# New slots in a hand-ordered plan: y times silu(z) and the norms' variances one slot later, plans of their own for the MLPs of images 5 to 7 and for the first unit

## The chip, the cores and the metric

The kernel runs on one NeuronCore of a Trainium2 chip. What counts is the device time of one execution in microseconds (us). It is told as the median of three runs, beside one execution that the hardware profiler recorded.

## What is computed

The input is a batch of 8 images of 384 channels and 32 x 32 pixels, in float32. Four layers follow one another. Layer 0 is a Mamba block with a residual. Layer 1 is a Mamba block whose output is scaled by a gate (attention pooling over the image, then two small products), with a residual, and then an MLP with a residual. Layers 2 and 3 are depthwise 13 x 13 convolutions with folded batch norms, and a pointwise product between them. Cut to what matters here:

```python
xn  = (x - mean) * rsqrt(var + 1e-5) * ln_w + ln_b       # norm over the 384 channels
xin, z = split(xn @ in_proj_w.T)                         # 768 channels each
u   = silu(conv4(xin) + conv_b)                          # causal, 4 taps
dt_lo, B, C = split(u @ x_proj_w.T)                      # 24 ranks, 16 + 16 states
delta = softplus(dt_lo @ dt_proj_w.T + dt_proj_b)
h   = h * exp(delta * A) + delta * u * B                 # a scan over 1024 pixels, 16 states
y   = (sum over states of h * C + u * D) * silu(z)
out = y @ out_proj_w.T + x
...
xs = xs + mo * (1 + mod)                                 # layer 1, behind its Mamba block
h  = gelu(ln(xs) @ fc1_w.T + fc1_b) @ fc2_w.T + fc2_b    # 384 -> 1536 -> 384
xs = xs + h
```

## The kernel before

**Units and items.** The work of both Mamba layers is cut into 32 units: a layer, an image and one half of its pixels (512). Their order is layer 0 of images 0 and 1, then alternately layer 1 of image b-1 and layer 0 of image b+1, and at the end layer 1 of images 6 and 7. Each unit has 48 items: 6 blocks of 128 channels (d) times 8 items (n), where an item is a tile of 128 x 1024 numbers (32 channels times 4 states on the partitions, two quarters of the channels along the free side). One slot of the plan belongs to one item, so scans run in slots 0 to 1535.

**What each slot issues.** The loop at the end of `layers` goes through the slots K. All engines' orders are written out by hand: within an engine, instructions run in the order in which the program issues them. In slot K the loop issues `fold` (every second slot: PE adds the two finished items K-2 and K-1 into `acc`, L574; with the first pair of a block also the product with D, L571), `keep` (ACT stores the last state, L560; for the items named in `AT["pool"]` POOL multiplies h by C, L563), `decay` of item K+1 (ACT, two exponentials, L516), `inflow` of item K+2 (POOL, L523), `scan` of item K (DVE, L544 or L547, and for the items not in `AT["pool"]` also h times C, L552), and then everything that the plan holds for slot K: first what was put with `first=True`, then the rest, each in the order in which it was put.

**Buffers that matter.** `hc`, the product of h and C, has 3 buffers in SBUF, used in turn by DVE's and POOL's products. `acc` is one PSUM buffer: L571 of the next block starts it anew, after `y_out` (L579, DVE, acc times silu(z)) has read the old one. `f`, for the MLP's products, is one PSUM buffer too: ACT has to take each one out (L690) before the next begins. `mm` has two PSUM buffers. `sq`, the square of the centred input, has one buffer.

**The plan.** `AT` is a table of slots. Unit i's preparation (norm, in-projection L406, shift and convolution L416 to L437, ranks L460, step sizes L482, z) stands in the slots of unit i-1; its output products (L595) in those of unit i+1. A norm is a chain: load (L361), mean on PE (L366), centring on DVE (L369), three squares on ACT (L375), each followed at once by its product with 1/384 on PE (L376), then ACT and POOL steps. Step sizes go to DRAM (`flat`, L496) and come back repeated over partitions (`repeat`, L505); both are DMAs of SP's queue.

**MLP.** Each half image passes through the MLP as one piece of the plan: a norm, 12 up slices of 3 products (L686) at `pace_up` slots each, four batches of gelu (L447), then 3 down outputs of 12 products (L699) at `pace_down` slots each. A half starts when the half before it is through and its unit has ended. `mlp_plan` has the numbers: (pace_up, first down slot, pace_down, slots of the gelu batches, gap). Before, plan 0 serves images 0 to 6, plans 2 and 3 the two halves of image 7, and plan 1 is not used.

**The first unit.** Negative slots come before the first scan, and there is nothing in them but the plan: the weights of the in-projection are multiplied by the norm's gain (`fold_product`, `fold_scale`, L343 to L353), stored to DRAM (`fold_store`, L356) and loaded from there by `slice_in` (L311), also for the first unit. Besides, `prepare` makes the filter tables of the convolutions in pieces, one to a slot from slot -40: batch norms, a bias regrouped through DRAM (`by_group` L140, `grouped` L145), `spread` (L150, PE and ACT), and six tables (loads L194, DVE, store L216).

Of the kernel before, what the change touches and what calls it, by code (L numbers as in the profile page):

```python
# [16 lines left out]
P = 128  # L17
# [93 lines left out]
def prepare(nc, k, vec, a, dram, tile, mm, got):  # L111
# [65 lines left out]
    yield  # L177
    for n, quad in zip(("b2", "b3"), quads):
        spread(n, quad)
    yield  # L180
# [4 lines left out]
    for name in ("k2", "k3"):  # L185
        got[name] = dram.tile([C, 4, HK, KP], F32, name=f"{name}_rows")
        for c in range(KC):
# [29 lines left out]
            yield  # L217

AT = {'in_ahead': 3, 'out_ahead': 2, 'taps_ahead': 4, 'norm': (-5, -2, -1, 0, 1, 2, 3, 3, 4, 5, 7, 8, 12, 12, 13), 'x': (14, 16, 18, 24, 26, 29), 'shift': 1, 'conv': 4, 'u': 5, 'silu': ((28, 3, 0), (34, 6, 0), (40, 6, 4), (57, 6, 6)), 'hid': 2, 'ranks': (33, 34, 35), 'z': (31, 35, 37, 38, 40, 41), 'B': (41, 43, 46, 47), 'C': (44, 46, 47, 50), 'repeat': (9, 12, 12, 13), 'out': (0, 4, 9), 'out_half': 3, 'out_add': 4, 'out_gate': 2, 'res_ahead': 1, 'heads': 15, 'softmax': (16, 17, 18), 'attend': (19, 24, 27, 26), 'context': 28, 'hidden': (28, 29, 32, 35, 36, 39), 'gates': (43, 40, 45), 'mlp': 22, 'mlp_norm': (-7, 0, 1, 1, 2, 3, 4, 4, 4, 6, 6, 10, 11, 11, 12), 'mlp_plan': ((3, 60, 12, (21, 33, 44, 69), -2), (1, 48, 7, (20, 24, 44, 48), -2), (2, 46, 6, (18, 30, 36, 46), -2), (1, 36, 4, (22, 30, 36, 36), -2)), 'fold0': (-22, -13), 'fold0_step': (1, 2), 'shifted': 1, 'bc_out': 36, 'store': 2, 'px_ahead': 2, 'pool': (0, 6), 'norm0': (-98, -18, -16, -15, -14, -13, -12, -11, -10, -10, -9, -8, -8, -3, -3), 'soft': ((37, 2), (45, 4), (62, 6)), 'du': 1, 'du_pace': 0, 'flat_u': 2, 'inject': 0, 'prepare': (-40, 4),
# [3 lines left out]
def layers(tc, k, a, vec, x0, x1, x2, x3, lasting, got):  # L225
# [11 lines left out]
    PIECES = 27  # L237
# [4 lines left out]
    with ExitStack() as st:  # L242
# [69 lines left out]

        def slice_out(s, m, src):
            s.w["out", m] = work.tile([P, KD, P], F32, tag="wo", name="wo", bufs=3)
            nc.sync.dma_start(s.w["out", m], src)
# [55 lines left out]
        def square(s, c):  # L371
            if c == 0:
                s.var = mm()
            sq = work.tile([P, T], F32, tag="sq", name="sq", bufs=1)
            nc.scalar.activation(sq, s.xt[:, c], AF.Square)  # L375
            nc.tensor.matmul(s.var, k["avg"], sq, start=c == 0, stop=c == KC - 1)  # L376
# [340 lines left out]
        def norm(s, src, tag, at, slots):  # L717
# [5 lines left out]
            for c in range(KC):  # L723
                put(next(slots), square, s, c)
# [18 lines left out]
        for j, s in enumerate(folds):  # L743
            for m in range(2 * KD):
                at = (j - 1) * SLOTS + 7 + 2 * m if j else AT["fold0"][m // KD] + AT["fold0_step"][m // KD] * (m % KD) - SLOTS
                use_in(at, s, m, s.src[m])
                put(at, fold_product, s, m)
                put(at + 1, fold_scale, s, m, first=True)
                put(at + 2, fold_store, s, m)

# [7 lines left out]
        for i, s in enumerate(units):  # L758

            lay, at = s.layer, (i - 1) * SLOTS  # L760
            norm(s, lay.src[s.b], "xt", at, AT["norm"] if i else AT["norm0"])
            for d in range(KD):
                e = at + AT["x"][d]
                use_in(e, s, d, lay.w_in[d])
# [7 lines left out]
            for j, (e, u1, z1) in enumerate(AT["silu"]):  # L772
# [3 lines left out]
                put(at + e, table, batch, AF.Silu)  # L776
                u0, z0 = u1, z1
            for e, d1 in AT["soft"]:
# [9 lines left out]
            put(at + AT["ranks"][0] - 6, load_xp, s)  # L788
            put(at + AT["ranks"][0], ranks, s, (0, 1, 2))
            put(at + AT["ranks"][1], ranks, s, (3, 4, 5))  # L790
            put(at + AT["ranks"][2], ranks_out, s, first=True)
            for d, e in enumerate(AT["z"]):
                use_in(at + e, s, KD + d, lay.w_in[KD + d])
                put(at + e, product, s, KD + d)
                put(at + e + 1, raw_z, s, d, first=True)
            put(at + AT["bc_out"], bc_out, s)
# [375 lines left out]
```

## Time and profile before

| | us |
|---|---|
| runs: median of 3 | 6992.39 |
| lowest, highest | 6982.28, 6993.99 |
| the profiled execution | 6987.24 |
| its span, first to last instruction | 6985.1 |
| TensorE's granted clock, mean | 0.919 |
| first scan starts | 142.56 |
| last y times silu(z) starts | 6120.42 |

The page gives, per engine, the time in which it was busy and its share of the span. A wait is named by the instruction that stood and by the one that released it, so `DVE u L579 <- PE acc L574` is DVE standing before line 579 until a product of line 574 was done; behind it stand the total, the number of times and the longest. In a window's line the first numbers are its bounds and length, then busy time (and count of instructions) of PE, PEld (weight loads), DVE, ACT and POOL, then TensorE's clock, the share of the DMA engines and GB/s.

### The profile page before, as it was taken

The page shows a single profiled execution, that of the slowest core. Times are in us where ns is not written, and L with a number is a line of the kernel's source. Part 1 is how long each engine was busy: PE and PEld are TensorE (multiplying, and loading weights), DVE is VectorE, ACT ScalarE, POOL GpSimd, SP SyncE. Part 2 cuts the span into 40 slices and gives each one's busy share as a digit, 9 for nine tenths or more (in the row PEclk, how much of TensorE's full clock was granted, in tenths as well). Part 3 has the DMA queues.
Part 4 walks back from the last instruction along what each step waited for, and adds up shares of the span by engine and source line. Part 5 has one row for each costly group of instructions (what it writes and reads, how often), then busy time and mean ns, then how long its engine had stood idle before and what let it go on. Part 6 is the DMA issues. An engine that isn't in the chain of part 4 may idle for free. (4 is left out here: it accounts for less than half of the span.)

```text
span 6985.1 us, 78481 instructions
## 1 busy us (share of the span) xinstructions
PE 5945.9 (85%) x22562; PEld 2089.5 (30%) x22562; DVE 5843.5 (84%) x4975; ACT 4472.7 (64%) x7478; POOL 5427.6 (78%) x3146
## 2 busy tenths in 40 slices
PE   6887787888888888889888888888888989777898
PEld 2222222222322232223222232223222323134545
DVE  3899998898888889888988989889998888903849
ACT  4776666767676767767676767676777767422222
POOL 2888888888898878888888888888888788804626
PEclk7888889999999999999999999999999999899999
DMA  5655555566656565666656665666565666425979
GB/s 141 173 166 156 153 163 149 162 168 173 174 160 180 154 181 162 168 163 173 165 163 166 169 180 160 171 167 181 158 176 164 174 163 171 131 67 139 263 223 241
DMA packets 962291, 1171.95 MB, mean 168 GB/s; under 512 B 314248, under 2 KB 554440, under 8 KB 961864
## 3 DMA queue, kind: packets, MB, share of 16 engines
q1 hardware_dynamic: 789576, 1064.75, 56.2%
q10 hardware_dynamic: 147712, 55.08, 3.0%
q0 software_dynamic: 24576, 47.12, 2.3%
q8 instruction: 184, 3.01, 0.2%
q14 instruction: 243, 1.99, 0.1%
HBM read 911.75 MB, written 204.21 MB: 160 GB/s over the span
## 5 line engine op out<-in xcount | busy, mean ns | idle before, releaser
L523 POOL TENSOR_TENSOR dbu<-B,ru 128x1024 f32<-128x1024 f32 x1536 | 3589.8, 2359 | 193.9 <-DVE h L547 75.9
L516 ACT ACTIVATE h<-rd,A 128x512 f32<-128x512 f32 x3072 | 2120.8, 691 | 826.2 <-DVE hc L552 613.1
L544 DVE TENSOR_TENSOR_SCAN h<-h,state,dbu 128x512 f32<-128x512 f32 x1152 | 1482.4, 1287 | 97.1 <-POOL delta L491 40.9
L552 DVE TENSOR_TENSOR hc<-h,C 128x1024 f32<-128x1024 f32 x1152 | 1411.1, 1225 | 110.7 <-PE acc L574 19.3
L547 DVE TENSOR_TENSOR_SCAN h<-h,dbu 128x1024 f32<-128x1024 f32 x576 | 1318.4, 2289 | 157.6 <-ACT h L516 127.8
L574 PE MATMUL acc<-hc,fold 128*32 128x512 f32 x6144 | 1152.9, 668 | 259.8 <-DVE hc L552 214.4
L563 POOL TENSOR_TENSOR hc<-dbu,C 128x1024 f32<-128x1024 f32 x384 | 904.0, 2354 | 529.2 <-DVE dbu L544 224.5
L406 PE MATMUL mm<-xt,wi 128*128 128x512 f32 x2304 | 1195.3, 660 | 94.8 <-ACT delta L482 25.7
L686 PE MATMUL f<-mx,wi 128*128 128x512 f32 x1152 | 625.6, 648 | 157.4 <-ACT fh L690 76.2
L699 PE MATMUL f<-fh,wo 128*128 128x512 f32 x1152 | 617.8, 648 | 116.9 <-DMA wo<-in_fc_dram 46.0
L406 PEld LDWEIGHTS mm<-xt,wi 128*128 128x128 f32 x2304 | 449.9, 207 | 821.8 <-issue 569.9
L595 PE MATMUL mm<-u,wo 128*128 128x512 f32 x1152 | 555.7, 620 | 30.1 <-DMA wo<-in_l_out_dram 28.3
L544 DVE TENSOR_TENSOR_SCAN dbu<-h,state,dbu 128x512 f32<-128x512 f32 x384 | 470.6, 1268 | 23.9 <-ACT h L516 14.2
L574 PEld LDWEIGHTS acc<-hc,fold 128*32 128x32 f32 x6144 | 163.4, 112 | 1091.3 <-DVE hc L552 482.7
L547 DVE TENSOR_TENSOR_SCAN dbu<-h,dbu 128x1024 f32<-128x1024 f32 x192 | 438.0, 2281 | 20.7 <-ACT h L516 11.2
L956 PE MATMUL ps<-xp,wt 128*32 128x256 f32 x6144 | 378.9, 389 | 61.0 <-DVE xp L951 37.9
L932 POOL DMA_DIRECT2D xp<-x x384 | 212.8, 558 | 278.5 <-DMA x<-q_out 139.2
L430 PE MATMUL mm<-xp,taps 128*64 128x512 f32 x1536 | 413.8, 661 | 17.9 <-ACT xp L416 9.6
L486 POOL TENSOR_TENSOR delta<-delta,u 128x512 f32<-128x512 f32 x192 | 241.2, 1266 | 231.4 <-ACT delta L482 228.8
L686 PEld LDWEIGHTS f<-mx,wi 128*128 128x128 f32 x1152 | 214.1, 202 | 541.7 <-issue 276.4
L306 ACT ACT_TABLE_LOAD x289 | 370.8, 1283 | 5.8 <-PEq L1160 0.7
L416 ACT ACTIVATE xp<-mm,b_in 64x512 f32<-64x512 f32 x384 | 261.7, 681 | 166.9 <-PE mm L406 163.0
(142 smaller groups left out, 5783.9 us busy)
## 6 DMA issues: line engine op xcount, KB each, us to landing
ru<-uu SPq DMA_DIRECT2D x1536, 128.0 KB
rd<-dd SPq DMA_DIRECT2D x1536, 128.0 KB
wi<-w_in SPq DMA_DIRECT2D x384, 192.0 KB
xp<-xp SPq DMA_DIRECT2D x384, 128.5 KB
dd<-delta SPq DMA_DIRECT2D x192, 256.0 KB
uu<-delta SPq DMA_DIRECT2D x192, 256.0 KB
wo<-in_l_out_dram SPq DMA_DIRECT2D x96, 384.0 KB
wi<-fc_w SPq DMA_DIRECT2D x192, 192.0 KB
```

Source lines behind the costliest of these rows:

```text
L406: nc.tensor.matmul(s.ps[m], w[:, c], s.xt[:, c], start=c == 0, stop=c == KC - 1)
L430: nc.tensor.matmul(s.ps[d][64 * h : 64 * h + 64], taps[:, h, j], xp[h][:, 2 * j : 2 * j + T], start=j == 0, stop=j == 1,)
L516: nc.scalar.activation(y[:, q], s.dr[d][1][h][:, q], AF.Exp, scale=s.layer.A[:, at : at + 1])
L523: nc.gpsimd.tensor_tensor(dbu, s.B[g].unsqueeze(1).to_broadcast([P, 2, T]), s.ur[d][1][h], ALU.mult)
L544: nc.vector.tensor_tensor_scan(to[:, q], y[:, q], dbu[:, q], first, ALU.mult, ALU.add)
L547: nc.vector.tensor_tensor_scan(flat_to, flat_y, flat_b, first, ALU.mult, ALU.add)
L552: nc.vector.tensor_tensor(hc, to, s.C[g].unsqueeze(1).to_broadcast([P, 2, T]), ALU.mult)
L563: nc.gpsimd.tensor_tensor(hc, y, s.C[g].unsqueeze(1).to_broadcast([P, 2, T]), ALU.mult)
L574: nc.tensor.matmul(s.acc[d][32 * r : 32 * r + 32], k["fold"], tiles[r // 2][:, r % 2], start=False, stop=n == PER - 2)
L595: nc.tensor.matmul(s.ps[m], w[:, d], s.us[d], start=d == 0, stop=d == KD - 1)
L686: nc.tensor.matmul(s.ps[m], s.w["in", m][:, c], s.xt[:, c], start=c == 0, stop=c == KC - 1)
L699: nc.tensor.matmul(s.down, s.w["out", 2 * m + f // KD][:, f % KD], s.hs[f], start=f == 0, stop=f == KF - 1)
```

## The change

The arithmetic is the same; the order and some buffers change.

- `y_out` is put at `AT["y"]` = 25 instead of 24: one slot later, after the second scan of the next block.
- POOL multiplies items 0 and 4 of each block by C, instead of 0 and 6.
- `square` is split: the product with 1/384 is now `variance`, put one slot after the square, ahead of the plan's other entries of that slot.
- `fold` is issued after the scan of the slot instead of at its start.
- `mlp_plan` gets five plans: images 0 to 4, image 5, image 6, and the two halves of image 7. `mlp_raw` is put at a slot computed otherwise, which is the same one for paces 1, 2 and 3.
- For the first unit, the twelve weight slices are loaded into buffers of `u` and `zs`, all at one early slot, scaled there and handed to the products from there (`slice_first`, `lend`); they are still stored to DRAM for later units. The first unit's preparation has a table of slots of its own (`first`, `norm0`), and the second unit's norm too (`norm1`). `prepare` has `spread` as its last piece, and one piece fewer.
- A number of other slots move by one or a few.

`AT` is a single line in the file; its changed entries are shown one to a line.

```diff
-'norm': (-5, -2, -1, 0, 1, 2, 3, 3, 4, 5, 7, 8, 12, 12, 13)
+'norm': (-5, -2, -1, 0, 1, 2, 3, 3, 5, 5, 7, 7, 11, 12, 13)
-'silu': ((28, 3, 0), (34, 6, 0), (40, 6, 4), (57, 6, 6))
+'silu': ((28, 3, 0), (34, 6, 0), (40, 6, 3), (57, 6, 6))
-'z': (31, 35, 37, 38, 40, 41), 'B': (41, 43, 46, 47), 'C': (44, 46, 47, 50)
+'z': (31, 34, 36, 38, 40, 41), 'B': (40, 43, 47, 48), 'C': (42, 45, 47, 52)
-'out': (0, 4, 9), 'softmax': (16, 17, 18), 'attend': (19, 24, 27, 26)
+'out': (0, 5, 9), 'softmax': (17, 18, 19), 'attend': (19, 22, 25, 26)
-'hidden': (28, 29, 32, 35, 36, 39), 'gates': (43, 40, 45)
+'hidden': (29, 30, 32, 35, 36, 39), 'gates': (47, 41, 46)
-'mlp_norm': (-7, 0, 1, 1, 2, 3, 4, 4, 4, 6, 6, 10, 11, 11, 12)
+'mlp_norm': (-7, 0, 1, 2, 3, 4, 5, 5, 5, 6, 6, 10, 10, 12, 12)
-'mlp_plan': ((3, 60, 12, (21, 33, 44, 69), -2), (1, 48, 7, (20, 24, 44, 48), -2),
-             (2, 46, 6, (18, 30, 36, 46), -2), (1, 36, 4, (22, 30, 36, 36), -2))
+'mlp_plan': ((3, 62, 12, (21, 31, 42, 69), -2), (2, 42, 6, (26, 30, 42, 46), -2),
+             (2, 40, 4, (24, 26, 34, 40), -2), (2, 40, 3, (24, 26, 34, 36), -2),
+             (2, 42, 7, (22, 28, 36, 36), -2))
-'fold0': (-22, -13), 'fold0_step': (1, 2), 'bc_out': 36, 'pool': (0, 6), 'flat_u': 2
+'fold0': (-145, -128), 'fold0_step': (1, 7), 'bc_out': 37, 'pool': (0, 4), 'flat_u': 1
-'norm0': (-98, -18, -16, -15, -14, -13, -12, -11, -10, -10, -9, -8, -8, -3, -3)
+'norm0': (-97, -89, -86, -85, -83, -80, -77, -75, -74, -73, -72, -71, -69, -69, -68)
+'norm1': (-3, -1, 0, 1, 2, 3, 4, 4, 8, 8, 10, 10, 12, 13, 13)
+'y': 25, 'fold': 0, 'var': 1, 'down_gap': 0
+'first': {'x': [2, 4, 7, 10, 13, 16], 'silu': [[14, 3, 0], [22, 6, 0], [34, 6, 2], [44, 6, 6]],
+          'ranks': [22, 24, 25], 'z': [29, 31, 31, 33, 34, 35],
+          'soft': [[29, 2], [33, 4], [60, 6]], 'bc_out': 29,
+          'B': [32, 34, 36, 39], 'repeat': [0, 0, 0, 1], 'C': [38, 43, 43, 46]}
```

```diff
 def prepare(nc, k, vec, a, dram, tile, mm, got):
...
     quads = [grouped(n, f) for n, f in zip(("b2", "b3"), flats)]
-    yield
-    yield
-    for n, quad in zip(("b2", "b3"), quads):
-        spread(n, quad)
     yield
...
             nc.sync.dma_start(got[name][c * P : (c + 1) * P], rows)
             yield
+    for n, quad in zip(("b2", "b3"), quads):
+        spread(n, quad)
+    yield
...
+        def slice_first(s, m, src):
+
+            tag, bufs = ("u", 12) if m < KD else ("zs", 7)
+            t = work.tile([P, T], F32, tag=tag, name=tag, bufs=bufs)
+            s.w["in", m] = t[:, 0 : KC * P].rearrange("p (c m) -> p c m", m=P)
+            nc.sync.dma_start(s.w["in", m], src)
...
         def square(s, c):
+            sq = work.tile([P, T], F32, tag="sq", name="sq", bufs=1)
+            nc.scalar.activation(sq, s.xt[:, c], AF.Square)
+            s.sq = {c: sq}
+
+        def variance(s, c):
             if c == 0:
                 s.var = mm()
-            sq = work.tile([P, T], F32, tag="sq", name="sq", bufs=1)
-            nc.scalar.activation(sq, s.xt[:, c], AF.Square)
-            nc.tensor.matmul(s.var, k["avg"], sq, start=c == 0, stop=c == KC - 1)
+            nc.tensor.matmul(s.var, k["avg"], s.sq.pop(c), start=c == 0, stop=c == KC - 1)
...
             for c in range(KC):
-                put(next(slots), square, s, c)
+                e = next(slots)
+                put(e, square, s, c)
+                put(e + AT["var"], variance, s, c, first=AT["var"] > 0)
...
-                at = (j - 1) * SLOTS + 7 + 2 * m if j else AT["fold0"][m // KD] + AT["fold0_step"][m // KD] * (m % KD) - SLOTS
-                use_in(at, s, m, s.src[m])
+                at = (j - 1) * SLOTS + 7 + 2 * m if j else AT["fold0"][m // KD] + AT["fold0_step"][m // KD] * (m % KD)
+                put(at - AT["in_ahead"] if j else AT["norm0"][0] - SLOTS, slice_in if j else slice_first, s, m, s.src[m])
...
+        def lend(s, m):
+            s.w["in", m] = folds[0].w["in", m]
...
-            norm(s, lay.src[s.b], "xt", at, AT["norm"] if i else AT["norm0"])
+            first = AT if i else {**AT, **AT["first"]}
+            norm(s, lay.src[s.b], "xt", at, AT["norm"] if i > 1 else AT[f"norm{i}"])
             for d in range(KD):
-                e = at + AT["x"][d]
-                use_in(e, s, d, lay.w_in[d])
+                e = at + first["x"][d]
+                if i:
+                    use_in(e, s, d, lay.w_in[d])
+                else:
+                    put(e, lend, s, d)
...
             for d in range(KD):
                 at = i * SLOTS + (d - 2) * PER
-                for e, (which, h) in zip(AT["repeat"], (("u", 0), ("d", 0), ("u", 1), ("d", 1))):
+                slots = AT["first"]["repeat"] if i == d == 0 else AT["repeat"]
+                for e, (which, h) in zip(slots, (("u", 0), ("d", 0), ("u", 1), ("d", 1))):
                     put(at + e, repeat, s, d, which, h)
                 put(at + 12, load_skip, s, d)
-                put(at + 24, y_out, s, d, first=True)
+                put(at + AT["y"], y_out, s, d, first=True)
...
-                pace_up, down, pace_down, tables, gap = AT["mlp_plan"][max(b - B + 2, 0) + (b == B - 1) * (1 + half)]
+                pace_up, down, pace_down, tables, gap = AT["mlp_plan"][max(b - B + 4, 0) + (b == B - 1) * half]
...
-                    put(e + pace_up, mlp_raw, s, m, first=True)
+                    put(e + 2 * pace_up // KC + 1, mlp_raw, s, m, first=True)
...
             for K in range(min(plan.slots), n_items + 1):
-                if K > 0 and K % 2 == 0:
-                    fold((item(K - 2), item(K - 1)))
...
                     scan(item(K))
-                plan.run(K)
+                if AT["fold"]:
+                    plan.run(K)
+                if K > 0 and K % 2 == 0:
+                    fold((item(K - 2), item(K - 1)))
+                if not AT["fold"]:
+                    plan.run(K)
```

## The prediction

> **What bounds the kernel now.** I read the page's busy shares first, then the chain of waits (to cut the span into stages), then the windows of those stages, the waits of each engine between the first and the last scan, and last the timeline around single waits.
>
> ```profile
> PE 5945.9 (85%) x22562; PEld 2089.5 (30%) x22562; DVE 5843.5 (84%) x4975; ACT 4472.7 (64%) x7478; POOL 5427.6 (78%) x3146
> ```
>
> Two engines are nearly full, so the stages decide. The timeline of DVE has the first scan at 142.56 and the last y times silu(z) (L579) at 6120.42. The windows (busy time of PE, PEld, DVE, ACT, POOL, then clock and DMA) of the prologue, of units 26 to 31 (each ends at its sixth L579) and of the three stretches after the last scan:
>
> ```profile
> 0.00:142.50 142.50, 94.82 (x240) 43.78 (x240) 27.55 (x121) 62.08 (x136) 17.91 (x24) 0.78 0.49 137
> ```
> ```profile
> 5003.30:5179.90 176.60, 153.89 (x470) 48.73 (x469) 159.19 (x98) 140.48 (x245) 154.76 (x75) 0.96 0.61 169
> 5179.90:5374.50 194.60, 167.24 (x487) 53.55 (x486) 172.75 (x145) 126.44 (x193) 163.06 (x84) 0.93 0.62 165
> 5374.50:5563.10 188.60, 169.84 (x553) 60.46 (x552) 168.38 (x122) 141.82 (x252) 155.02 (x75) 0.92 0.65 176
> 5563.10:5757.30 194.20, 169.64 (x491) 54.23 (x490) 173.09 (x145) 128.41 (x196) 163.11 (x84) 0.92 0.62 166
> 5757.30:5942.30 185.00, 167.94 (x545) 58.90 (x544) 166.64 (x121) 143.23 (x254) 155.02 (x75) 0.92 0.62 171
> 5942.30:6120.40 178.10, 125.63 (x328) 33.16 (x326) 168.60 (x143) 82.85 (x118) 142.37 (x66) 0.81 0.46 123
> ```
> ```profile
> 6120.40:6204.00 83.60, 71.64 (x157) 29.63 (x158) 5.20 (x7) 20.03 (x26) 0.00 (x0) 0.98 0.33 83
> 6204.00:6308.00 104.00, 77.75 (x158) 29.98 (x156) 4.44 (x4) 28.85 (x38) 7.88 (x7) 0.90 0.28 71
> 6308.00:6408.00 100.00, 73.56 (x152) 27.54 (x150) 2.86 (x5) 28.85 (x38) 37.26 (x46) 0.95 0.33 83
> ```
>
> The reader is to see three regimes: 142.5 us in which no engine is full; 5978 us of scans, DVE about 90% busy and PE close behind; and 288 us of MLP alone (6120 to 6408), where DVE and POOL stand still. The 577 us of depthwise convolutions behind are untouched. What DVE waits for between 142 and 6120 (us in total, times, longest):
>
> ```profile
> DVE u L579 <- PE acc L574: 172.4, 89, 5.8
> DVE h L547 <- ACT h L516: 127.8, 83, 3.0
> DVE h L544 <- POOL delta L491: 40.9, 30, 3.4
> ...
> DVE hc L552 <- PE acc L574: 19.3, 30, 2.4
> ```
>
> The first is the costliest, and the timeline shows one of its causes:
>
> ```profile
> 3021.92 2.07 PE L376 MATMUL mm<-sq,avg 128*128 128x512 f32 x2 [3.56 <-ACT sq L375]
> ...
> 3023.93 1.94 PE L574 MATMUL acc<-hc,fold 128*32 128x512 f32 x8
> ...
> 3025.93 0.69 DVE L579 TENSOR_TENSOR u<-acc,zs 128x512 f32<-128x512 f32 x1 [2.42 <-PE acc L574]
> ```
>
> PE stood 3.56 us before a variance product, since ACT had not yet squared; the fold queued behind it ended late, and DVE stood 2.42 us before L579. PE loses 110.4 us to this wait in the scans (L376 on L375).
>
> **What the Trainium skill says.** "TensorE: Matmul & The Clock Gate", Part 2, Step-by-step: matmuls stay in program order, only weight loads are pulled ahead; the three lines above agree, the fold did not pass the waiting variance. "Perfetto Trace Analysis", Identifying the Most-Contended Engine: busy matmul time is a poor measure of distance from PE's limit. So I take a unit with 91% (167.94 of 185.00) as nearly full, not as full. "DMA: Bandwidth & Descriptors", Two DMAs through the same engine are not ordered: a DMA that reads what another wrote must wait for its completion. SP does so here, standing from 48.3 (a load of taps comes between) to 55.5:
>
> ```profile
> 46.88 0.90 SPq L140 DMA_DIRECT2D b_flat<-fh  x2
> ...
> 55.53 0.93 SPq L145 DMA_DIRECT2D fh<-b_flat  x2
> ```
>
> **Part 1: y one slot later, POOL's products at items 0 and 4, variance one slot later.** No instruction is added. L579 moves behind scan 1 and product hc 1 of the next channel block. It cannot gain a whole slot: hc has 3 buffers, and hc 1 reuses that of hc 6, which the same fold frees. So DVE will wait for that fold at hc 1 (L552). That comes one scan (2.29 us, L547) later than L579 did. Listing the 90 waits of L579 (173.6 us over the whole trace), the part up to 2.3 us of each sums to 141.6, and 32 remain. More of the cause goes too: POOL's hc 6 no longer stands before this fold (PE waits 42.8 us for L563), and the 110 us before variances. The moved wait of the variance itself has 3.9 us (5978/1536 items) more to be met. Against it: acc is one buffer, so the skip product (L571, two records of 0.59, 1.2 us) of the next block now waits for L579 (0.68) behind hc 1, where it ran early. Behind it on PE stand the fold of items 0 and 1 and whatever the plan has. Where PE was waiting for hc 1 anyway this delays PE 0.68 + 1.2 = 1.9 us per block; where PE is late, nothing. Its 192 blocks bound it by 365 us, and by 0. I take 60 us given back, between the two: PE waits for DVE at L574 159 times, but most such moments have slack behind them. Net -80, range -140 to +100. The fold call's new place behind the scan changes no engine's order (only fold and plan issue to PE). flat_u one slot earlier makes SP wait for POOL's product sooner; L496 waits 162 us for it now without DVE waiting for the result (no DMA among DVE's main waits); the other moved slots I cost at 0 with it.
>
> **Part 2: MLP plans of images 5, 6, 7.** By the code's arithmetic the halves start at slots 1222, 1318, 1414, 1510, 1606, 1668 before; after at 1222, 1280, 1414, 1464, 1514, 1561. Scans end at 1536. Before, one half and its ups from slot 1536 on, then two more halves lie behind; after, one half less: the half that ran from 6204 to 6308 moves under scans, 104 us. What stands at 6120 is otherwise the same (5 of 12 ups done, the same output products). Besides, 4 of the down products before it follow the last norm's mean, not 2: 2 x 0.95 us more of that norm hidden. Sum -106, range -98 to -114.
>
> The displaced work: a half is 36 up and 36 down products of 0.95 us and 9 of the norm, 77 us. Spread over slots by each plan's pace (34 us over the ups, 34 over the downs, 9 at the start) it changes the PE load of units 25 to 31 by about +7, +27, +19, -34, -13, +38, +31. Unit 26: 154 + 27 = 181 in 176.6, so some +13; unit 27 +2; unit 30: 168 + 38 = 206, at 96%, which no window shows yet, about 215, +30; unit 31: 157 in 178, +2; units 28 and 29 relieved, -10 each. Sum +27, range 0 to +60.
>
> **Part 3: the first unit.** The twelve weight slices stay in SBUF (buffers of u and zs), so the products no longer wait for a round trip through w_in (4.5, 3.7 and 0.9 us at L406), and spread, for which PE stood 10.5 us, goes to the end. Against it, 12 x 0.45 us of slice loads now precede x in SP's queue: x lands about 19 instead of 14, the norm ends about 44 instead of 39. Then SP decides. The slots put the loads and stores of five of the six filter tables (7.9, 7.9, 7.7, 7.1, 5.8 us each in SP's timeline, L194 to L216) ahead of the flats. Product 3 ends about 65 (44 + 4 x 3.3 of L406 at the early clock + 2 x 2.5 of L430 + 3 for the first shift to land); SP meets the round trip (8.6 us) and starts the tables near 76; 5 of them, 36 us: the first flat at 112, against 114.85. From there to the scan it was 27.7 us, of which 9.8 SP stood before the third ru and a 768 KB load of the next x competed; both now come later, and I count 13. First scan at 125: -18, range -35 to 0.
>
> **Sum** against the profiled run (6987.24; its span 6985.1): -80 - 106 + 27 - 18 = -177, 6810. The median of the runs, 6992.4, lies 5 above that run, inside their spread of 12, so I say 6810.
>
> **Rivals.**
> - The wait merely moves (L579's 173 becomes L552's, or PE cannot run above 91%): part 1 gives -25. For it: L552 waits for the same fold. Against: DVE comes there 2.3 us later, and most waits are shorter. 6987 - 25 - 106 + 27 - 18 = 6865.
> - PE saturates in units 26, 27, 30, 31 and the displaced half comes back: crowding +80 instead of +27. For it: 206 of load in 185. Against: units 28 and 29 are idle enough. 6987 - 80 - 106 + 80 - 18 = 6863.
> - Everything hidden: nothing given back by the skip product (-140), crowding +10, start -30: 6987 - 140 - 106 + 10 - 30 = 6721.
> - Slower: the skip product. If PE is the bound in steady units and every block costs it 1.9 us: +365 - 142 = +223; 6987 + 223 - 106 + 27 - 18 = 7113. It decides once the give-back exceeds 142 + 106 + 18 - 27 = 239 us, 1.24 us per block. For it: PE's 91%. Against: PE idles 17 to 27 us per unit in the windows of 26 to 30, and the wait costs only where PE was ahead.
>
> That the change does not act is excluded: the slots are executed as written.
>
> **How the numbers follow.** Forecast 0.50, first rival 0.20, second 0.13, all hidden 0.10, slower 0.07. Range 6715 to 6890: it takes in the cases at 6721, 6865 and 6863 with the ends of the start and tail terms, and leaves out the slower one. What a measurement can tell from no change is 0.2%, 14 us. Faster 0.91, same 0.02, slower 0.07.
>
> **What would show it.** Right: L579 waits under 40 us, L552 on acc 30 to 80; L376's wait on L375 nearly gone; last L579 to the last MLP store about 182 us; unit 30 longer than 200; first scan near 125. Wrong: L571 waiting for L579 by hundreds of us with DVE waits growing elsewhere; a tail above 200; a first scan after 142, with SP standing at the filter tables.

## The result, and the profile after

The changed kernel takes 6950.82 us (median of 4 runs, 6940.02 to 6954.78), the kernel before 6991.66 in the same series (6982.28 to 6993.99). The ratio is 0.9942 with an interval of [0.9924, 0.9959]: about 41 us or 0.6% faster, where 6810 was forecast. The time lies above the upper end of the range, 6890. The profiled execution took 6954.78 us, its span 6952.9, at a mean clock of 0.926.

The busy line of the page of after, to be held against that of before:

```profile
PE 5904.4 (85%) x22562; PEld 2097.6 (30%) x22562; DVE 5851.6 (84%) x4975; ACT 4475.0 (64%) x7478; POOL 5429.7 (78%) x3146
```

The same work is done, and the two full engines stand at the same shares. The stages tell more. Windows of after (bounds, length, then busy PE, PEld, DVE, ACT, POOL, clock, DMA): the prologue, units 26 to 30, and the stretch behind the last y times silu(z), which starts at 6196.99:

```profile
0.00:133.30 133.30, 92.36 (x234) 42.96 (x234) 26.43 (x121) 65.57 (x141) 22.01 (x25) 0.81 0.44 130
...
5026.90:5230.70 203.80, 180.56 (x521) 60.37 (x521) 162.60 (x101) 146.00 (x253) 163.02 (x83) 0.92 0.63 165
5230.70:5427.70 197.00, 178.58 (x527) 59.62 (x526) 171.76 (x144) 139.13 (x209) 156.59 (x78) 0.95 0.64 166
5427.70:5616.30 188.60, 161.00 (x489) 54.93 (x487) 167.97 (x122) 125.48 (x229) 154.22 (x75) 0.83 0.61 166
5616.30:5805.60 189.30, 159.31 (x462) 48.87 (x462) 171.41 (x143) 131.52 (x201) 162.12 (x85) 0.94 0.59 158
5805.60:6021.30 215.70, 197.24 (x619) 72.29 (x620) 174.15 (x126) 149.91 (x265) 164.03 (x83) 0.94 0.65 169
...
6197.00:6280.00 83.00, 73.74 (x162) 30.42 (x162) 6.94 (x8) 26.27 (x35) 0.00 (x0) 0.98 0.33 86
6280.00:6372.50 92.50, 71.85 (x144) 27.99 (x144) 1.50 (x2) 26.15 (x34) 34.78 (x41) 0.91 0.34 79
```

Cutting both spans at the first scan and at each unit's sixth y gives the ledger, in us:

| stage | before | after | difference | prediction |
|---|---|---|---|---|
| prologue, to the first scan | 142.56 | 133.30 | -9.3 | -18 |
| unit 0 | 184.1 | 203.9 | +19.8 | 0 |
| units 1 to 25 | 4676.7 | 4689.7 | +12.9 | -80 |
| units 26 to 31 | 1117.1 | 1170.1 | +53.0 | +27 |
| last y to the last MLP output (L705, L714 after) | 287.5 | 175.5 | -112.0 | -106 |
| the rest | | | +3 | 0 |
| span | 6985.1 | 6952.9 | -32.2 | -177 |

The tail came as worked out. The steady units gave nothing (their +13 us is less than what a sum of 25 units differs by from one profile to the next, as the last section shows). Yet the wait on which their gain was put is gone. Waits of after between the first scan and the last y (waiting engine and line, releaser: us in total, times, longest). L588 is the old L579, L553 and L556 are the scans, L561 hc, L580 the skip product, L379 the square, L385 the variance:

```profile
DVE h L556 <- ACT h L525: 182.4, 111, 5.8
...
PE acc L580 <- DVE u L588: 153.5, 84, 4.9
ACT sq L379 <- PE mm L385: 151.6, 62, 5.4
...
DVE h L553 <- ACT h L525: 79.6, 44, 4.5
...
DVE xt L375 <- PE mm L372: 20.9, 4, 20.0
...
DVE hc L561 <- PE acc L583: 14.5, 14, 2.3
...
PE mm L385 <- ACT sq L379: 8.2, 8, 2.0
```

VectorE's 173.5 us before y are down to 1.2, and TensorE's 110.4 us before variances are down to 8.2. In their place VectorE waits 262 us for ScalarE's decays (L553 and L556 together; 163 before, L544 and L547), TensorE 153.5 us before the skip product (1.7 before), and ScalarE 151.6 us before squares (14.3 before). The lines named h leave out the scans of the two items that GpSimd multiplies by C, whose output is named dbu; with them VectorE waits 300 us for decays where it waited 189. Another 69 us before scans (2 before) have no releaser in the profile. In units 1 to 25 all of VectorE's waits sum to 387 us before and 386 us after: there the wait for y went elsewhere in full.

ScalarE's wait before squares is new in kind, and the timeline of after shows one case (start, duration, engine and line, then the idle time before it and its releaser):

```profile
3030.84 0.62 ACT L379 ACTIVATE sq<-mx 128x512 f32<-128x512 f32 x1
3032.13 1.42 ACT L525 ACTIVATE h<-rd,A 128x512 f32<-128x512 f32 x2 [0.67 <-DVE hc L561]
3037.61 0.63 ACT L379 ACTIVATE sq<-mx 128x512 f32<-128x512 f32 x1 [4.06 <-PE mm L385]
...
3032.75 1.90 PE L580 MATMUL acc<-u,skip 128*128 128x512 f32 x2 [4.44 <-DVE u L588]
3034.58 1.93 PE L583 MATMUL acc<-hc,fold 128*32 128x512 f32 x8
3036.44 1.13 PE L385 MATMUL mm<-sq,avg 128*128 128x512 f32 x2
```

TensorE stood 4.44 us for y, so the variance behind the fold came at 3036.44. It frees the only `sq` buffer, and ScalarE stood 4.06 us before the next square, with the next decay queued behind it (3038.14). Two of the edits meet here: y late holds up TensorE, the variance late ties ScalarE to TensorE. VectorE did not stand for that decay at once, though: its scans at 3036.40 and 3040.25 started without a wait. So this case shows how ScalarE is held, and not yet that VectorE's waits for decays come from it.

### The profile page after: what moved, and what is told of

Read it like the earlier page. It is cut to its first block, busy times and chain, and to the rows that moved or that the text cites. A ratio compares the mean times of both kernels' runs of the same rounds, so it can differ in the third digit from the quotient of the medians.

```text
span 6952.9 us, 78464 instructions
## 1 busy us (share of the span) xinstructions
PE 5904.4 (85%) x22562; PEld 2097.6 (30%) x22562; DVE 5851.6 (84%) x4975; ACT 4475.0 (64%) x7478; POOL 5429.7 (78%) x3146
## 5 line engine op out<-in xcount | busy, mean ns | idle before, releaser
L553 DVE TENSOR_TENSOR_SCAN h<-h,state,dbu 128x512 f32<-128x512 f32 x1152 | 1482.4, 1287 | 221.1 <-ACT h L525 79.6
L561 DVE TENSOR_TENSOR hc<-h,C 128x1024 f32<-128x1024 f32 x1152 | 1410.8, 1225 | 129.2 <-PE acc L583 14.5
L556 DVE TENSOR_TENSOR_SCAN h<-h,dbu 128x1024 f32<-128x1024 f32 x576 | 1318.1, 2288 | 239.0 <-ACT h L525 182.4
L583 PE MATMUL acc<-hc,fold 128*32 128x512 f32 x6144 | 1174.6, 663 | 340.7 <-DVE hc L561 257.9
L415 PE MATMUL mm<-xt,wi 128*128 128x512 f32 x2232 | 1123.3, 642 | 43.6 <-ACT delta L491 18.9
L695 PE MATMUL f<-mx,wi 128*128 128x512 f32 x1152 | 610.5, 638 | 139.9 <-ACT fh L699 111.0
L708 PE MATMUL f<-fh,wo 128*128 128x512 f32 x1152 | 587.0, 628 | 82.0 <-DMA wo<-in_fc_dram 66.8
L415 PEld LDWEIGHTS mm<-xt,wi 128*128 128x128 f32 x2232 | 424.7, 202 | 745.4 <-issue 447.8
L604 PE MATMUL mm<-u,wo 128*128 128x512 f32 x1152 | 579.4, 643 | 38.5 <-DMA wo<-in_l_out_dram 31.4
L553 DVE TENSOR_TENSOR_SCAN dbu<-h,state,dbu 128x512 f32<-128x512 f32 x384 | 470.4, 1267 | 14.0 <-ACT h L525 8.6
L556 DVE TENSOR_TENSOR_SCAN dbu<-h,dbu 128x1024 f32<-128x1024 f32 x192 | 437.9, 2281 | 39.8 <-ACT h L525 29.3
L305 ACT ACT_TABLE_LOAD x289 | 370.8, 1283 | 5.9 <-PEq L1186 0.7
L580 PE MATMUL acc<-u,skip 128*128 128x512 f32 x384 | 226.8, 675 | 153.7 <-DVE u L588 153.5
```

What stands on the lines that cost most here:

```text
L415: nc.tensor.matmul(s.ps[m], w[:, c], s.xt[:, c], start=c == 0, stop=c == KC - 1)
L553: nc.vector.tensor_tensor_scan(to[:, q], y[:, q], dbu[:, q], first, ALU.mult, ALU.add)
L556: nc.vector.tensor_tensor_scan(flat_to, flat_y, flat_b, first, ALU.mult, ALU.add)
L561: nc.vector.tensor_tensor(hc, to, s.C[g].unsqueeze(1).to_broadcast([P, 2, T]), ALU.mult)
L583: nc.tensor.matmul(s.acc[d][32 * r : 32 * r + 32], k["fold"], tiles[r // 2][:, r % 2], start=False, stop=n == PER - 2)
L604: nc.tensor.matmul(s.ps[m], w[:, d], s.us[d], start=d == 0, stop=d == KD - 1)
```

## The experiments

Theory at the outset: part 1 of the change does not take waiting out of the loop but hands it on, from VectorE to ScalarE's decays and to the skip product, and the late variance adds a wait instead of taking one away. Rival: the steady units are as worked out, and what ate the gain is the crowding by the MLP and the first unit. All kernels are the changed one with some edit, or the one before with some edit; medians in us. Each ratio is to runs of the kernel before in the same series. Their medians lie between 6985.9 and 6992.0, so a difference between medians of two series is good to some 6 us.

| run | median | ratio to before, interval |
|---|---|---|
| after, y at 24 | 6983.72 | 0.9987 [0.9979, 0.9996] |
| after, variance in its square's slot | 6918.27 | 0.9895 [0.9878, 0.9911] |
| after, items (0, 6) on GpSimd | 6960.31 | 0.9953 [0.9939, 0.9968] |
| after, squares in two buffers | 6933.10 | 0.9916 [0.9901, 0.9930] |
| before, y at 25 | 6943.66 | 0.9930 [0.9912, 0.9947] |
| after, image 5 on plan 0 | 6934.02 | 0.9914 [0.9899, 0.9930] |
| after, x of unit 1 loaded 9 slots sooner | 6926.03 | 0.9916 [0.9898, 0.9933] |
| repaired: variance, image 5 and x together | 6881.32 | 0.9848 [0.9827, 0.9868] |
| before without table switches, y at 24 | 6741.91 | 0.9656 [0.9636, 0.9676] |
| the same, y at 25 | 6732.83 | 0.9636 [0.9620, 0.9652] |
| before with all five new MLP plans | 6961.12 | 0.9966 [0.9953, 0.9979] |
| repaired, steady slots of before | 6934.59 | 0.9928 [0.9913, 0.9943] |
| before, y at 25 and items (0, 4) | 6975.63 | 0.9984 [0.9977, 0.9990] |
| repaired, slots of before, items (0, 6) | 6894.41 | 0.9867 [0.9852, 0.9883] |
| repaired, y at 24 | 6958.81 | 0.9956 [0.9939, 0.9972] |
| repaired, items (0, 6) | 6903.44 | 0.9880 [0.9864, 0.9897] |
| repaired, slots of before, (0, 6), plan 0 of before | 6870.58 | 0.9833 [0.9818, 0.9847] |
| before with the plans of images 5 to 7 only | 6937.50 | 0.9925 [0.9909, 0.9942] |

### What y's slot is worth

```diff
-'y': 25
+'y': 24
```

After with y back at 24:

> The changed kernel with y times silu(z) back at slot 24. Theory A (the wait is only handed on: with y at 25 DVE waits as long elsewhere): units 1 to 25 within 15 us of the changed kernel's 4704, though DVE waits for the fold at y again (over 80 us). Theory B (y at 25 gains what was predicted, some 80 us, and another part of the change gives it back): units 1 to 25 longer by 50 to 100 us.

It is 33 us slower than after: 123 us of VectorE's wait at L588 are back, and the wait at the skip product is gone (1.5 us). Units 1 to 25 take 4701.5 us, 12 more than the ledger's 4689.7 (the text above has 4704 for it), as theory A has it. The edit is good, but it is worth 33 us for a wait of 123.

```diff
-put(at + 24, y_out, s, d, first=True)
+put(at + 25, y_out, s, d, first=True)
```

Before, with this alone:

> The kernel before with one edit: y times silu(z) at slot 25. Theory A (handed on): DVE's wait for the fold at y goes from 173 to under 60 us, its waits for ACT's decays grow by most of that, and the time falls by under 30 us (within 0.4%). The prediction's step: the time falls by 60 to 100 us.

It gains 48 us, in units 1 to 25 38 us (4638.9 against 4676.7), of a wait of 173.5. That lies between the two expected ranges. Its waits between first scan and last y:

```profile
DVE h L547 <- ACT h L516: 175.6, 119, 3.7
...
PE acc L571 <- DVE u L579: 153.6, 105, 4.9
...
DVE h L544 <- ACT h L516: 47.4, 51, 2.3
```

Of the 173.5, 60 are back in VectorE's waits for decays (223 against 163; 270 against 189 with the scans named dbu), and TensorE now stands 153.6 us before the skip product, on average 0.80 us in each of 192 blocks. The decays may be late because of ScalarE's table switches. The timeline of this kernel shows one such burst:

```profile
3061.37 1.28 ACT L447 ACT_TABLE_LOAD   x1
3062.66 2.19 ACT L447 ACTIVATE zs<-zs 128x512 f32<-128x512 f32 x4
3064.87 1.28 ACT L306 ACT_TABLE_LOAD   x1
3066.16 1.42 ACT L516 ACTIVATE h<-rd,A 128x512 f32<-128x512 f32 x2
```

For 4.8 us no decay is made, and the scan at 3067.68 waited 2.31 us for this one. The Trainium skill, "ScalarE: Activation LUTs", What ACT_TABLE_LOAD costs, gives about 1283 ns for a load, and the trace agrees (1.28 us here, 1283 ns mean). It adds a drain of about 1380 ns to every switch; no drain is seen here, where the activation before ends 0.02 us ahead of each load and the next one starts 0.01 us behind it. So I formed the theory that these bursts take what the slot of y fails to bring, and took the switches away, and with them the functions that need them. What is left out is silu, gelu and softplus, so these two kernels compute something else:

```diff
 for t in ts():
-    nc.scalar.activation(t, t, f)
-exp_ln()
+    nc.scalar.activation(t, t, AF.Identity)
...
-nc.scalar.activation(s.delta[d], ps, AF.Softplus)
+nc.scalar.activation(s.delta[d], ps, AF.Exp)
```

> The kernel before, y times silu(z) still at slot 24, with ScalarE's table switches taken out: silu and gelu are replaced by identity on the same tiles and softplus by exp, and the preload behind each batch is gone, so that part of the computation is left out; the count of ScalarE operations on tiles is the same. It is the base for the next run. Theory (the bursts of ScalarE, in which each switch costs 1.28 us, are what VectorE falls back on once it no longer waits for y): the kernel gets faster than before by 100 to 350 us, VectorE's wait for y at L579 stays at 150 to 200 us, and its waits for ScalarE's decays at L544 and L547 fall from 163 us to under 80. Rival (VectorE falls back on TensorE's order alone, the accumulator that the skip product waits for): these waits for decays stay near 163.

> The same kernel without ScalarE's table switches (silu and gelu as identity, softplus as exp), with y at slot 25. With the switches, the one slot was worth 48 us. Theory (ScalarE's bursts took the rest of the 173 us wait): without them the slot is worth clearly more, 90 to 170 us between this kernel and the one of the run beside it. Rival (the rest was taken by the skip product L571, which waits for y and holds up the accumulator): it is worth 20 to 60 us as before, and VectorE waits for TensorE at hc L552 instead.

The waits, first of the kernel without switches at y 24, then at y 25 (lines are two lower here: L577 is y, L569 the skip product, L545 a scan):

```profile
DVE u L577 <- PE acc L572: 145.1, 93, 5.6
...
DVE h L545 <- ACT h L514: 45.3, 50, 1.6
```

```profile
PE acc L569 <- DVE u L577: 116.8, 84, 4.9
DVE h L545 <- ACT h L514: 98.6, 69, 4.0
...
DVE hc L550 <- PE acc L572: 49.4, 42, 5.4
```

The first half of the theory held: without switches the kernel is 244 us faster and the waits for decays fall (163 us to 46 at y 24). The second fell: the slot of y is worth 9 us, not 90 to 170, and 9 us is hardly clear of the spread of the runs (6734 to 6767 at y 24, 6731 to 6735 at y 25). Its 145 us again turn into 117 us of TensorE before the skip product and 69 us more of VectorE before decays (115 at L542 and L545 together, after 46). The rival's range (20 to 60) missed too, on the low side, and its wait at hc did not grow (59.5 us to 49.4). The switches cost time, but they are not what swallows the gain. What is common to both pairs is that VectorE's wait for TensorE comes back as TensorE's wait for VectorE and as VectorE's wait for decays. Which path makes the decays late, and why the slot is worth more in one setting than in another, was not isolated; a second `acc` buffer, which would end the wait at the skip product, was not tried.

Last, y at 24 in the repaired kernel (below):

> The repaired kernel (6881 us) with y back at slot 24: what the one slot of y is worth when the variance is not late. In after it is worth 33 us, in before 48 us, with ScalarE's switches taken out 9 us. If its worth is what is left over between VectorE's wait and TensorE's new wait at the skip product, it is again 20 to 50 us here (6900 to 6930 us), with VectorE waiting 110 to 170 us for the accumulator at L588 and TensorE's wait at L580 gone from 90 us to under 10.

Here the slot is worth 77 us, more than the 50 expected at most; VectorE waits 123.5 us at L588, and the wait at L580 is gone. So the same edit is worth 9, 33, 48 or 77 us, depending on what stands beside it.

### The variance one slot later

```diff
-'var': 1
+'var': 0
```

> The changed kernel with the variance product again in the slot of its square. Theory B1 (the variance a slot later makes ACT stand 159 us before squares, because sq has one buffer, and that takes y's gain back): units 1 to 25 shorter by 30 to 80 us, ACT's wait at squares under 40 us. Theory A: within 15 us, PE standing some 100 us before variances again.

After gains 33 us by undoing it, units 1 to 25 30 us (4660.0), at the lower end of theory B1. Its waits:

```profile
PE acc L580 <- DVE u L588: 91.1, 65, 4.9
...
PE mm L385 <- ACT sq L379: 68.6, 36, 3.5
...
ACT sq L379 <- PE mm L385: 30.8, 13, 5.7
```

ScalarE's wait falls from 151.6 to 30.8 us, that at the skip product from 153.5 to 91.1; TensorE's before the variance rises by 60 only. VectorE's waits for decays stay where they were (263 us at L553 and L556, 262 in after): the late variance is not what makes the decays late. To see whether the single `sq` buffer makes the cost, the square of channel block 1 went to a buffer that is idle then, with the variance still late:

```diff
-sq = work.tile([P, T], F32, tag="sq", name="sq", bufs=1)
+sq = work.tile([P, T], F32, tag=("sq", "rs_v")[c % 2], name=("sq", "rs_v")[c % 2], bufs=1)
```

> The changed kernel with squares taking turns in two buffers (sq and rs_v), so a square need not wait for the variance before it. Theory B1: ACT's wait at squares falls from 159 to under 60 us and units 1 to 25 are shorter by 30 to 80 us. Theory A: ACT's wait falls as well, units 1 to 25 within 15 us.

ScalarE's wait is gone (2.9 us), but the time falls by 18 us only, of it 7 in units 1 to 25, where the theory of the buffer asked for 30 to 80, and the skip product still waits 168.4 us. So the buffer is half of the cost at most. The rest is not isolated; the skip product's wait, which falls to 91.1 us only when the variance is back in its slot, points to TensorE's order.

### Items on GpSimd, and the steady slots

```diff
-'pool': (0, 4)
+'pool': (0, 6)
```

> The changed kernel with POOL's products at items 0 and 6 again. Theory B2 (items 0 and 4 cost what y gained): units 1 to 25 shorter by 30 us or more. Theory A: within 15 us. If items 0 and 4 help: longer, and DVE waits for the fold at hc again, since the last fold of a block then waits for POOL.

In after, (0, 4) is worth 9 us, which is within the spread of the runs (6940 to 6955 against 6955 to 6965); units 1 to 25 hardly differ (4691.9 us for 4689.7). The repaired kernel was then given the old rows of the plan (`norm`, `silu`, `z`, `B`, `C`, `bc_out`, `flat_u`, `softmax`, `attend`, `hidden`, `gates`, `out`, `mlp_norm`):

> After with the variance in the slot of its square, image 5 on the ordinary plan, the load of the second unit's image at slot -12 (the three repairs together), and besides these the steady slots of before (norm, silu, z, B, C, flattening of du, softmax, attention, gates, out-projection). If the new steady slots cost time too, as units 1 to 25 at 4660 us in the repaired kernel against 4639 us in before with y at 25 alone suggest, this run is 15 to 40 us below the 6881 us of the repaired kernel, and ScalarE's wait for the repeated delta (100 us in after, 31 in before) falls to under 50. If the new slots are worth having, it is 10 to 50 us above 6881.

It became 53 us slower, so the new rows seemed worth having, against what the steady units of before with y at 25 (4639 us) had suggested. That contradiction led to (0, 4) itself, first in before with y at 25, then under the old rows, then under the new ones:

> The kernel before with y at slot 25 and with items 0 and 4 of a block on GpSimd in place of 0 and 6: the two edits on which part 1 of the prediction put its gain, and nothing else. If items (0, 4) are worth the 9 us that they are worth among the new slots, this is 6930 to 6940 us, against 6944 us with y at 25 alone. If (0, 4) only suits the new slots, and explains why the repaired kernel with the old slots came out at 6935 us, this is 6965 us or more, and units 1 to 25 take over 4660 us (4639 us with y at 25 alone).

> After with the three repairs and the old steady slots of before (6935 us), now with items (0, 6) on GpSimd, as before had them. If items (0, 4) are what costs time with the old slots, units 1 to 25 fall from 4691 us to about 4640 us and the time to 6870 to 6890 us. If something else of after does, it stays within 10 us of 6935 us.

> The repaired kernel (6881 us) with items (0, 6) on GpSimd. If (0, 4) suits the new slots, as in after, it is 5 to 20 us slower, 6886 to 6901 us; if the repairs have changed that, it is the same or faster.

The edits that the prediction credited with 80 us, y and (0, 4), bring 10 us against the kernel before when they are made alone, where y alone brought 48: (0, 4) costs 32 us by the medians and 38 by the ratios. The repaired kernel gives the whole square (all with y at 25, variance in its slot, new plan 0):

| | items (0, 6) | items (0, 4) |
|---|---|---|
| rows of before | 6894.41 | 6934.59 |
| rows of after | 6903.44 | 6881.32 |

Neither edit has a worth of its own: (0, 4) costs 40 us with the old rows and brings 22 with the new; the new rows bring 53 us with (0, 4) and cost 9 with (0, 6). The 9 and the 22 are hardly clear of the spread (the runs of a cell lie up to 30 us apart), the 40 and the 53 are. Which row makes the difference was not tried, and the waits do not show it: in before with y at 25, (0, 4) raises VectorE's waits for decays from 223 to 281 us in the scans named h, but lowers them from 47 to 5 in those named dbu, since other items now carry that name. The sum goes from 269.7 to 285.5.

### The MLP plans

```diff
-'mlp_plan': (plan_0, (2, 42, 6, (26, 30, 42, 46), -2), ...)
+'mlp_plan': (plan_0, plan_0, ...)
```

> The changed kernel with image 5's MLP on the plan of images 0 to 4. If PE is overfilled in unit 26 (180.6 us of products in 203.8): unit 26 back to about 177, units 28 and 29 up to 194 at most, the tail unchanged; 20 to 30 us faster than the changed kernel. If unit 26 is long for another reason: within 8 us.

Image 5 back on plan 0 brings 17 us, somewhat less than expected, and unit 26 is 178.3 us instead of 203.8. Unit 30 stays long, at 217.8 (215.7 in after). Next, all five plans in the kernel before:

> The kernel before with the five MLP plans of after alone (images 5, 6 and both halves of 7), everything else at its old slot: part 2 by itself. If the parts add up as in the profiled executions of before and after, the tail behind the last y shortens by 105 to 112 us, units 26 to 31 get longer by 45 to 60 us together (unit 26 by 20 to 30, unit 30 by 25 to 40), and the kernel is 45 to 65 us faster than before, so more than the whole change. If the crowding came from the new slots beside it and not from the plans, units 26 to 31 get longer by 10 to 30 us and the kernel is 80 to 100 us faster.

It gains 25 us, half of what was expected, and the windows show where the rest went. Units 0 to 5 have the lengths of before to 0.1 us. Units 6 and 7 of before, then of this run:

```profile
1241.90:1421.40 179.50, 156.80 (x470) 49.42 (x469) 159.02 (x98) 140.79 (x245) 154.86 (x75) 0.93 0.61 166
1421.40:1614.70 193.30, 167.15 (x485) 53.07 (x484) 172.85 (x145) 126.54 (x193) 163.08 (x84) 0.93 0.61 167
```

```profile
1241.80:1418.40 176.60, 151.34 (x466) 48.28 (x465) 158.28 (x97) 140.80 (x245) 154.90 (x75) 0.98 0.59 168
1418.40:1615.10 196.70, 166.47 (x491) 53.87 (x490) 173.53 (x147) 126.60 (x193) 163.06 (x84) 0.96 0.61 165
```

A few products have moved from unit 6 (470 to 466) to unit 7 (485 to 491); unit 6 gets 2.9 us shorter and unit 7 3.4 longer. Further on the odd units lose more than the even ones gain (units 15 and 17: 194.8 to 198.5 and 190.8 to 197.1), and units 1 to 25 sum to 4704.3, 28 us longer. The suspect is plan 0, which serves images 0 to 4: its down products start at 62 instead of 60 and two gelu batches sit 2 slots earlier. Two runs separate it:

```diff
-(3, 62, 12, (21, 31, 42, 69), -2)
+(3, 60, 12, (21, 33, 44, 69), -2)
```

> The kernel before with new MLP plans for images 5, 6 and both halves of 7 only; plan 0, which serves images 0 to 4, stays as before. This is what the prediction called part 2. If plan 0 is what made units 6 to 25 longer by 28 us in the run with all five plans, units 1 to 25 are now as before (4677 us, within 3), the tail behind the last y is 105 to 112 us shorter, units 26 to 31 are 45 to 65 us longer, and the time is 6925 to 6945 us.

> The kernel with the three repairs, the old steady slots and items (0, 6) (6894 us), now with plan 0 of the MLP as before had it (down products from slot 60, gelu batches at 33 and 44) in place of after's plan 0 (62, 31, 42). Plan 0 serves images 0 to 4, so it acts in all steady units. With the five new plans alone in the kernel before, units 0 to 5 had the same lengths as before to 0.1 us, and units 6 to 25, where plan 0 acts, were 28 us longer. Theory (the new plan 0 costs this among the old slots): units 1 to 25 fall by 15 to 35 us and the time to 6860 to 6880 us. Rival (those 28 us came from y at 24 beside it): within 8 us of 6894 us.

Without the new plan 0, part 2 alone gives 6937.5 (53 us gained): units 1 to 25 4671.8, 5 shorter than before where 3 were allowed; the tail 111 shorter; units 26 to 31 61 longer, of it unit 26 18 and unit 30 38. Between the two runs on before, plan 0 costs 24 us (6961.12 to 6937.50), and in the other pair 24 as well (6894.41 to 6870.58). So the cost appears in two surroundings and the theory holds, though it does not sit in the same place: units 1 to 25 are 33 us longer in the first pair and 18 in the second (4647.5 to 4630.0). Under the new rows it was not measured. One wait goes with plan 0 in both pairs: ScalarE's before decays, for the repeated delta that a DMA brings. With all five new plans, then with the plans of images 5 to 7 only:

```profile
ACT h L516 <- DMA rd<-dd: 66.6, 27, 5.4
```

```profile
ACT h L516 <- DMA rd<-dd: 28.2, 18, 3.4
```

In the other pair it is 79.2 us with the new plan 0 and 22.8 with the old. Before has 31.0 and after 100.3, and the old rows alone took it only from 110.4 (repaired) to 86.0. How two slots of the MLP delay a delta was not followed.

### The first unit, and the repairs together

```diff
-'norm1': (-3, -1, 0, ...)
+'norm1': (-12, -1, 0, ...)
```

> The changed kernel with the load of the second unit's x nine slots earlier in SP's order. If DVE's 20 us before the centring of unit 1 come from that load's place behind SP's waits: unit 0 shrinks from 204 to about 185, 10 to 20 us faster. If DMA is simply full there: the load only takes from the repeats, first scan later by as much, within 8 us.

The timeline of after, in which the x of unit 1 is issued at 136.40 (123.86 before: `norm1` itself puts it two slots later) and VectorE meets its centring right behind the first scan (start 133.30). Before, VectorE centred it ahead of its first scan, in time in which it had nothing else to do:

```profile
136.40 0.48 SPq L367 DMA_DIRECT2D xt<-in_x_dram  x1
...
150.07 5.46 PE L372 MATMUL mm<-xt,avg 128*128 128x512 f32 x6 [23.83 <-DMA xt<-in_x_dram]
...
155.57 1.75 DVE L375 TENSOR_TENSOR xt<-xt,mm 128x1536 f32<-128x1536 f32 x1 [19.98 <-PE mm L372]
```

The scan came 9 us sooner, the load 12.5 us later: nearly 20 us of unit 0 are a wait for it. Issued sooner (at 127.16), that wait is 4.9 us, unit 0 is 191.9 instead of 203.9 (about 185 was expected), and the time is 25 us lower. Unit 0 has 12 of these; the rest lies in units whose program is the same, and no run explains it.

> The changed kernel with the variance in the slot of its square, image 5 on the old plan and the earlier load of unit 1's x. The three add if they are independent: 33 + 25 + 15 us below the changed kernel's 6951, about 6878. If they share one cause: not below 6905.

The three repairs bring 70 us together (33 + 17 + 25 = 75 one by one). The fastest kernel of the study with the whole computation takes 6870.58 us: y at 25, the early x, the first unit's own plan and the new plans of images 6 and 7 on the old rows, (0, 6), the old plan 0, and the variance behind its square. Made alone in the kernel before, y's slot brought 48 us and the plans of images 5 to 7 brought 53; the whole change brought 41.

## Why the prediction was wrong

The direction and the stage of the surest gain were right, and the size was wrong by 145 us of the profiled span. By its own steps:

- **Part 1, "Net -80": failed.** This is the step that carries most of the miss (93 us: +13 for -80 in units 1 to 25). Its mechanism, that a wait of VectorE turns into one of TensorE at the skip product, was right, and four of its terms were wrong. First, what comes back: it took 141.6 us as gained and 60 as given back by the skip product. With y's slot alone, TensorE's new wait there was 154 us, and VectorE's waits for decays, a term that the prediction put at nothing, grew by 60 to 81 us. The slot brought 48 us, 38 of them in units 1 to 25. Second, the items (0, 4) were counted as relief; alone with y they cost 32 us. Third, the late variance was counted as relief; it cost 33 us in after, where TensorE's 110 us of waiting went and ScalarE's 152 came (of the cost, the buffer explains half at most). Fourth, "the other moved slots I cost at 0" held neither for the rows (53 us gained with one choice of items, a few lost with the other) nor for plan 0, whose edit the prediction did not name and which cost 24.
- **The rival "the wait merely moves"** had the right outcome for units 1 to 25 and the wrong place. Its sign at hc was 14.5 us, not 173: the wait moved to TensorE at L580 and to decays.
- **The slower rival, the skip product,** had the right mechanism and stayed below its point of decision: 153.5 us over 192 blocks is 0.80 us a block, where 1.24 was needed.
- **Tail, -106: right** (-112; 175.5 us left where about 182 was expected).
- **Crowding, +27: right mechanism, size off** (+53). Unit 30 came as worked out (+31 for +30), in part by luck: it had 197 us of products where 206 were reckoned, and was busy for 91% of its length where 96% was taken. Unit 26 gave +27 for +13. TensorE is busy there for 180.56 of 203.80 us: the load, 181, was right, but the prediction added only what went beyond the old length, as if TensorE could be busy throughout. Units 30 and 26 run at 91% and 89%, about the 91% read in unit 30 of before; that quotient was the one to divide by. Not all of unit 26 is the plan's doing: with the plans of images 5 to 7 alone in the kernel before, it took 194.8 us. Units 28 and 29 gave back 5 us together, not 20. The products did leave unit 28 (489 records of products, 553 before), but TensorE was busy only 9 us less there, at a granted clock of 0.83 where before had 0.92.
- **First unit, -18: wrong.** The scan started at 133.30, not 125, and unit 0 became 20 us longer, a stage to which the prediction gave no term. The first flat left at 107.61, sooner than the 112 worked out; the term that failed is the 13 us from there to the scan, which were 25.7. The prediction reckoned with SP and the DMAs there, and the timeline shows ScalarE. For unit 0, the prediction had noted that the next x comes later, and took that as relief for SP; it did not ask who waits for that x.

In the kernel before, ScalarE stood 10.23 us for a repeat ahead of its first decay. In after it comes to that decay straight from z, with two batches of silu and four table loads since 121.38, and does not stand:

```profile
128.28 2.19 ACT L456 ACTIVATE zs<-zs 128x512 f32<-128x512 f32 x4
130.48 1.28 ACT L305 ACT_TABLE_LOAD   x1
131.78 2.75 ACT L525 ACTIVATE h<-rd,A 128x512 f32<-128x512 f32 x4
```

No run moved that batch, so this is read from one timeline.

## What to carry to other kernels

Where several engines run in step through single buffers, a wait in a profile is not the price of removing it: here 173.5 us brought 48, since the engine that had been waited for began to wait in turn. Before an edit is credited, name for each instruction that is moved who reuses its buffer next; a square that is freed one slot later gave ScalarE a longer wait than it took from TensorE. And price a table of slots as a whole: the same choice of items cost 40 us or brought 22 when its neighbours changed, so single edits have to be measured in the surroundings in which they will stand.

## What the runs showed of the hardware

Two programs that differ only from unit 6 on (before, and before with all five new plans) gave units 0 to 5 equal to 0.1 us each (184.0, 186.7, 174.2, 180.5, 183.1, and 190.8 against 190.7 in the windows). That is not the rule: before and the kernel with the plans of images 5 to 7 only are the same up to unit 24, and single units differ by up to 3.1 us. After and the kernel with the early x are the same from unit 2 on, and their units 2 to 25 sum to 4508.5 and 4488.1. So a difference of 5 us in a unit of one profile can be read, one of 3 can't, and a sum of 25 units can't be read below some 20 us; the medians of the runs decide.

Table switches took 740 us of ScalarE's busy time (577 loads of 1283 ns), on an engine that is 64% busy. Without them the kernel was 244 us faster, so an engine far from full can still set the pace by when it is busy.
